# Sorted rows and normalised rows turned by VectorE behind block-wise loads, in a fused convolution-attention and expert-routing kernel

## The chip, the cores and the metric

The kernel runs on one core of one Trainium2 chip. The metric is the device time of one execution in microseconds (us). TensorE multiplies and transposes matrices into PSUM; VectorE, ScalarE and GpSimd work elementwise; SyncE issues most of the DMA transfers that move data between DRAM and SBUF; 16 DMA engines carry them. In profile rows these engines are called PE (with PEld for its weight loads), DVE, ACT, POOL and SP.

## The reference

The input `x` has 4 images of 32 channels, 128 x 128. Everything is float32.

Layer 0 is a channel attention. Each image becomes a matrix q of 128 channels by 4096 places:

```python
xs = x.reshape(B, C, h, R, w, R).transpose(0, 1, 3, 5, 2, 4).reshape(B, C * R * R, h, w)   # R = 2
...
energy = jnp.einsum('bci,bcj->bij', q, q)
d = jnp.sqrt(jnp.diagonal(energy, axis1=1, axis2=2))
energy = energy / (d[:, :, None] * d[:, None, :])
attn = jax.nn.softmax(energy, axis=-1)
out = jnp.einsum('bcj,bij->bci', q, attn).reshape(B, C * R * R, h, w)
out = gamma * out + xs
```

Layer 1 reads the result as tokens of 128 values. The linear attention and the experts follow, each on layer-normalised tokens and each added to the tokens:

```python
t = t + _L1_attn_ref(_ln_t(t), L1_attn_Wk, L1_attn_Wq, L1_attn_Wv)
t = t + _L1_ffn_ref(_ln_t(t), L1_ffn_router_w, L1_ffn_router_b, L1_ffn_expert_w, L1_ffn_expert_b)
```

`_L1_ffn_ref` is a router with a softmax over 8 experts; each token takes the best two, multiplies by each one's 128 x 128 weights and adds the two results, weighted.

## The kernel before

The four images are worked off one after the other. `attend` walks over the 4096 x 4096 matrix of an image in blocks of 128 x 512. Each step has a product for the energies (`pe`, line 609), an exponential by ScalarE (`pr`, L612), a product of the exponential with values (`po`, L497) and, since the matrix is symmetric, a product of the transposed block (`pg`, L433). The transposed block is made without TensorE: VectorE turns `pr` in squares of 32 x 32 (L421, tile `F`), the block goes to DRAM (`move`, L530, tensor `blocks`) and comes back with its 32-row groups swapped (`swap_groups`, L545, `F<-blocks`, six DMAs). The product with it is given out 57 units of a clock after the swap (`LAG`), where one whole step counts 12 units.

Layer 1 of image b is worked in the gaps of the attention of image b + 1. It is written as Python generators (`layer1`): each `yield` is a half step, and the main loop takes one half step of that stream for every 10 units of the clock (`PACE`). So the order of instructions on TensorE, VectorE, ScalarE and SyncE is fixed by the program, and every engine works its own list from top to bottom.

Parts of layer 1 that matter here, for images 0 to 2:

- `close_rows(kc)`, four groups of 8 token rows: divides by the sums, adds to the tokens `T`, normalises them into `xn` (L696) and adds up their Gram matrix (`pgram`, L728). `stagger` starts a group every 6 half steps. The first group waits until the layer 1 of the image before is `sorted`.
- `matrix()`: makes one 128 x 144 matrix, `matx`, of the attention weights and the Gram matrix.
- `attention_rows(u)`, four groups: TensorE transposes the normalised rows, four 128 x 128 tiles at a time, into PSUM (`transpose_rows`, `ptx`, L701), ScalarE copies them out (`keep_rows`, `xnT`, L714), and TensorE multiplies them with `matx` (`pat`, L854). Then come the second normalisation and the router.
- `sorted_experts(h)`, for each half of an image: GpSimd scatters the normalised tokens to a DRAM tensor `xs` sorted by expert, with each token's weight in column 128 (L1053; rows are `DW` = 132 wide), in `NT` = 39 tiles of 128 tokens. The tiles are loaded in pairs (L1083), transposed by TensorE (`pys`, L1124), copied out by ScalarE (L1093), multiplied by their expert's weights (L1117), scaled with the token's weight by VectorE (L1099) and stored to `ys` (L1103). GpSimd then gathers the two results of each token (L1165).

Image 3 has no successor to hide in: it takes another way through layer 1 (`alone`, `last_parts`), with dense experts and with `transpose_rows`, too. The same tile tag names one set of buffers: `wide` and `grp` have two each.

TensorE's PSUM banks are handed out by `hold`, which gives back the function that empties the bank.

Of the kernel before, what the change touches and what calls it, by code (L numbers as in the profile page):

```python
# [22 lines left out]
def kernel(  # L23
# [43 lines left out]
    nc = tc.nc  # L67
    P = 128
# [3 lines left out]
    CH = 512  # L72
# [4 lines left out]
    S = 32  # L77
    NH, KQ, D = wk.shape
# [40 lines left out]
    DW = D + 4  # L119
# [71 lines left out]
    def hold(name, evict, alloc=psum_t):  # L191


        while len(held) >= banks[0]:
            held[0]()
        bank = alloc(name)

        def done():
            if done in held:
                held.remove(done)  # L200
                evict(bank)

        held.append(done)
        return bank, done
# [449 lines left out]
    def layer1(b, st):  # L654
# [43 lines left out]
        def transpose_rows(g):  # L698
            pt, done = hold(f"ptx_{b}_{g}", partial(keep_rows, g))
            for j in range(4):  # L700
                nc.tensor.transpose(pt[:, ts(j, P)], xn[:, 4 * g + j, :D], ident)  # L701
            return done

        def keep_rows(g, pt):

            if not alone:
                xnT = work.tile([P, CH], F32, tag="grp", name=f"xnT_{b}_{g}", bufs=2)
            else:
                nm = f"xnT_{b}_{g}"
                if g in (0, 2, 6):  # L710
                    pool, tag = (xin, "xx") if g == 0 else (qpool, "qT")
                    keep["two"] = pool.tile([P, 2, CH], F32, tag=tag, name=nm)
                xnT = npool.tile([P, CH], F32, tag="qn", name=nm) if g in (4, 5) else keep["two"][:, g % 2]
            nc.scalar.activation(xnT, pt, AF.Copy)  # L714
            keep[g] = xnT

# [14 lines left out]
        def close_rows(kc):  # L731
# [9 lines left out]

            while "exps" not in st if last_rows else missing():
                yield from idle(1)
            while b > 0 and kc == 0 and not states[b - 1].get("sorted"):
                yield from idle(1)
            den, rd = (stat.tile([P, 2 * NJ], F32, tag=nm, name=f"{nm}_{b}_{kc}") for nm in ("den", "rd"))
            nc.vector.tensor_reduce(den, st["sums"][:, ts(kc, 2 * NJ), :], AX.X, ALU.add)
# [174 lines left out]
        def transpose_tokens(g, alloc=psum_t):  # L922
# [7 lines left out]
                nc.tensor.transpose(pt[:, ts(j, P)], xn[:, 4 * g + j, :D], ident)  # L930
            return done

        def attention_rows(u):

            for g in (2 * u, 2 * u + 1):
                yield
                done = transpose_rows(g)
                yield
                done()
            la = stat.tile([P, 8, 2 * E], F32, tag="la", name=f"la_{b}_{u}")  # L940
            for j0 in range(0, 8, 3):
# [24 lines left out]
            if u % 2:  # L966
                for _ in route(u // 2):
                    yield
                    yield
                yield  # L970
                yield
                yield from sorted_experts(u // 2)

        def sorted_experts(h):
# [104 lines left out]
            def rows_of(dram_rows, g, n):  # L1079
                return dram_rows[2 * g * P : (2 * g + n) * P, :].rearrange("(j p) d -> p j d", p=P)  # L1080
# [6 lines left out]
            def products(turned, applied):  # L1087


                def leave(p):  # L1090
                    if turned:
                        g, n = turned
                        nc.scalar.activation(  # L1093
                            bufs[6 + g % 2][:, :n, :D], p[:, : n * P].rearrange("p (j t) -> p j t", t=P), AF.Copy
                        )
                    if applied:
                        g, n = applied
                        result = keep["results"][:, g % 4]
                        nc.vector.tensor_tensor(  # L1099
                            result[:, :n], p[:, 2 * P : 2 * P + n * D].rearrange("p (j c) -> p j c", c=D),  # L1100
                            bufs[g % 6][:, :n, D : D + 1].to_broadcast([P, n, D]), ALU.mult,
                        )
                        nc.sync.dma_start(rows_of(ys, g, n), result[:, :n])  # L1103

                p, done = hold(f"pys_{b}_{h}_{(turned or applied)[0]}", leave)
                if applied:
                    g, n = applied
                    if g % 2 == 0:
                        _, at = nc.values_load_multi_w_load_instructions(
                            begin[0:1, h, 2 * g : min(2 * g + 4, NT)], engines=[mybir.EngineType.PE], min_val=0,  # L1110
                            max_val=(E - 1) * D,
                            skip_runtime_bounds_check_because="D times a count of at most E - 1, never negative",
                        )
                        begins[:] = at
                    weights = ew_sb.rearrange("p e c -> p (e c)")
                    for j in range(n):
                        nc.tensor.matmul(  # L1117
                            p[:, 2 * P + j * D : 2 * P + j * D + D], bufs[6 + g % 2][:, j, :D],
                            weights[:, bass.ds(begins[2 * (g % 2) + j], D)], start=True, stop=True,
                        )  # L1120
                if turned:
                    g, n = turned
                    for j in range(n):
                        nc.tensor.transpose(p[:, ts(j, P)], bufs[g % 6][:, j, :D], ident)  # L1124
                return done

            if "results" not in keep:
                keep["results"] = work.tile([P, 4, 2, D], F32, tag="df", name=f"results_{b}", bufs=1)
            done = None
            begins = []  # L1130
            for at in range(len(pairs) + 5):
                if at < len(pairs):
                    load(*pairs[at])
                if done:
                    done()
                yield
                turned, applied = (pairs[at - d] if 0 <= at - d < len(pairs) else None for d in (3, 4))
                done = products(turned, applied) if turned or applied else None
                yield
            if done:  # L1140
                done()
            if h == 1:
                st["sorted"] = True
            yield from idle(1)
# [353 lines left out]
```

## Time and profile before

| What | Value |
|---|---|
| median of 3 runs | 1652.24 us (1652.22 to 1652.25) |
| the profiled execution's own time | 1659.2 us |
| its span, first to last instruction | 1657.4 us |
| TensorE busy | 1623.1 us, 98% of the span |
| VectorE busy | 917.4 us, 55% |
| ScalarE busy | 910.4 us, 55% |
| GpSimd busy | 596.2 us, 36% |
| DMA packets | 241899, 332.81 MB |
| packets under 512 bytes | 31984 |
| granted clock of TensorE, mean | 0.996 |

A group row of the profile names a line of the kernel, the engine, the operation, `out<-in` by tile names, the shapes and the count. After the bar stand the busy time in us (overlapping instructions counted once), the mean ns of one instruction, and the time that the engine was idle just before, with what ended it. A row of the waits reads: who waited, for whom, us in total, times, longest. The page's strips of 40 digits cut the span into 40 slices, with tenths of busy time. A window row gives, for a stretch of time, each engine's busy us and number of instructions.

### The profile page before, as it was taken

How to read it: one execution, taken by the hardware profiler on the slowest of the kernel's cores; microseconds unless marked ns; L12 is line 12 of the kernel's file. 1: busy time of each engine (PE TensorE's matmuls, PEld its weight loads, DVE VectorE, ACT ScalarE, POOL GpSimd, SP SyncE). 2: the span in 40 equal slices, each digit the busy share in tenths (PEclk: the TensorE clock that was granted, in tenths of full speed). 3: DMA queues.
4: the chain of work that ended last, by engine and by line, in shares of the span. 5: the costliest groups of instructions: out<-in, count | busy, mean ns of one | idle time of the engine just before them, and what ended most of it. 6: DMA issues, size and time to landing. Idle time of an engine off the chain costs nothing.

```text
span 1657.4 us, 21471 instructions
## 1 busy us (share of the span) xinstructions
PE 1623.1 (98%) x5288; PEld 856.9 (52%) x5288; DVE 917.4 (55%) x2359; ACT 910.4 (55%) x2863; POOL 596.2 (36%) x565
## 2 busy tenths in 40 slices
PE   8999999999999999999999999999999999999987
PEld 5444544455554455555564455555565445554643
DVE  4543353567486443559378453448559533344686
ACT  3555445566575555556575455556657455555376
POOL 1000000001014531456555543346546642436166
PEclk9999999999999999999999999999999999999999
DMA  4555656665349776986778868797668877885001
GB/s 147 199 181 174 198 186 213 230 212 170 131 171 277 246 220 213 271 249 176 207 200 254 265 208 255 214 287 200 167 196 239 277 222 246 240 254 168 15 14 39
DMA packets 241899, 332.81 MB, mean 201 GB/s; under 512 B 31984, under 2 KB 168304, under 8 KB 227440
## 3 DMA queue, kind: packets, MB, share of 16 engines
q1 hardware_dynamic: 207312, 291.92, 55.5%
q0 software_dynamic: 26624, 25.58, 7.5%
q10 hardware_dynamic: 7840, 13.93, 2.8%
q8 instruction: 45, 0.74, 0.2%
q14 instruction: 78, 0.64, 0.1%
HBM read 160.78 MB, written 175.80 MB: 203 GB/s over the span
## 4 chain that ended last, share of the span: by engine, by line
PE 84%; DMA 4%; DVE 4%; SPq 3%; ACT 2%; issue 2%; another core or an unknown queue 1%; POOL 0%; ACTq 0%; DVEq 0%; POOLq 0%
PE po L497 24%; PE pe L609 23%; PE pg L433 20%; PE pys L1117 3%; DMA blocks<-F 3%; PE py L1290 3%; PE pg L453 2%; SPq L545 2%; PE pat L854 2%; PE pys L1124 2%; PE pgram L728 1%; PE ptx L701 1%; DVE df L761 1%; PE pgv L839 0%
## 5 line engine op out<-in xcount | busy, mean ns | idle before, releaser
L612 ACT ACTIVATE pr<-pe 128x512 f32<-128x512 f32 (+1 forms) x576 | 322.4, 560 | 544.0 <-PE pe L609 448.2
L497 PE MATMUL po<-pr,qT 128*128 128x512 f32 (+3 forms) x1152 | 549.6, 559 | 4.2 <-ACT o L502 3.0
L609 PE MATMUL pe<-qn,qn 128*128 128x512 f32 x896 | 459.6, 595 | 2.6 <-ACT pr L612 1.6
L433 PE MATMUL pg<-F,qT 128*128 128x512 f32 x880 | 449.7, 592 | 1.1 <-DMA F<-blocks 1.1
L421 DVE STREAM_TRANSPOSE F<-pr 128x512 f32<-128x512 f32 x440 | 305.9, 702 | 144.8 <-ACT pr L612 127.0
L497 PEld LDWEIGHTS po<-pr,qT 128*128 128x128 f32 x1152 | 215.3, 190 | 251.7 <-issue 221.2
L1165 POOL DMA_INDIRECT acc<-ys,place x128 | 203.2, 1588 | 215.8 <-ACT pr L612 140.3
L438 ACT ACTIVATE junk<-F 128x512 bf16<-128x512 f32 x440 | 273.0, 620 | 1.2 <-DMA F<-blocks 1.2
L433 PEld LDWEIGHTS pg<-F,qT 128*128 128x128 f32 x880 | 166.7, 190 | 195.4 <-issue 181.0
L1053 POOL DMA_INDIRECT xs<-xn,place x192 | 186.0, 969 | 189.7 <-ACT pr L612 116.6
L609 PEld LDWEIGHTS pe<-qn,qn 128*128 128x128 f32 x896 | 155.0, 191 | 115.0 <-issue 104.6
L442 DVE TENSOR_TENSOR o<-o,pg 128x512 f32<-128x512 f32 x110 | 75.3, 684 | 207.9 <-PE pg L433 173.4
L1099 DVE TENSOR_TENSOR results<-pys,xn 128x256 f32<-128x256 f32 x120 | 49.9, 416 | 187.1 <-ACT xn L1093 122.0
L164 POOL TENSOR_TENSOR rn<-ss,neg_half 128x8 f32<-128x8 f32 (+1 forms) x17 | 27.2, 1602 | 320.9 <-DVE ss L296 320.8
L612 ACT ACTIVATION_READ_ACCUMULATOR pr<-pe 128x1 f32 x576 | 112.0, 194 | 0.0
L1093 ACT ACTIVATE xn<-pys 128x256 f32<-128x256 f32 x120 | 45.2, 377 | 112.5 <-PE pys L1124 94.5
L1117 PEld LDWEIGHTS pys<-ew_sb,xn 128*128 128x128 f32 x468 | 70.4, 191 | 53.0 <-issue 49.5
L1165 POOL DMA_INDIRECT yb<-ys,place x64 | 61.8, 965 | 84.5 <-DMA F<-blocks 31.1
L609 PE MATMUL pe<-qn 128*128 128x512 f32 (+3 forms) x256 | 90.2, 435 | 0.7 <-ACT qn L342 0.7
L438 ACT ACTIVATION_READ_ACCUMULATOR junk<-F 128x1 f32 x440 | 84.6, 192 | 0.0
L1117 PE MATMUL pys<-ew_sb,xn 128*128 x468 | 71.7, 275 | 0.4 <-ACT xn L1093 0.4
L164 POOL TENSOR_TENSOR rsa<-dm_a,neg_half 128x8 f32<-128x8 f32 x16 | 28.9, 1807 | 103.1 <-DVE sv_a L688 102.9
(216 smaller groups left out, 1521.1 us busy)
## 6 DMA issues: line engine op xcount, KB each, us to landing
blocks<-F SPq DMA_DIRECT2D x110, 1024.0 KB
F<-blocks SPq DMA_DIRECT2D x220, 192.0 KB
F<-blocks SPq DMA_DIRECT2D x220, 128.0 KB
xn<-xs SPq DMA_DIRECT2D x114, 132.0 KB
ys<-results SPq DMA_DIRECT2D x114, 128.0 KB
F<-blocks SPq DMA_DIRECT2D x220, 64.0 KB
below<-F SPq DMA_DIRECT2D x31, 384.0 KB
T<-in_x_dram SPq DMA_DIRECT2D x64, 128.0 KB
```

What stands on the lines that cost most here:

```text
L164: pinned(nc.gpsimd.tensor_tensor(dst, src, neg_half.to_broadcast(list(src.shape)), ALU.pow))
L421: f()
L433: nc.tensor.matmul(pg.rearrange("p (a f) -> p a f", a=4), st["qT"][i][:, ib, :], G[:, :, ib], start=(ib == 0), stop=(ib == NJ - 1),)
L438: nc.scalar.activation(junk, G[:, :, ib], AF.Copy, accum_out=st["sums"][:, NJ * i + ib, jc : jc + 1])
L442: nc.vector.tensor_tensor(st["o"][jc], st["o"][jc], pg, ALU.add)
L497: nc.tensor.matmul(row["po"][:, lo:hi], qT[blk // NJ][:, blk % NJ, :], w, start=start, stop=(row["left"] == 0))
L609: nc.tensor.matmul(pe[:, c0:], qn[jc][:, ts(j, P)], qn[i][:, c0:], start=True, stop=True)
L612: nc.scalar.activation(pr[:, c0:], pe[:, c0:], AF.Exp, accum_out=sums[:, t, i : i + 1]).ins
L1053: inst = nc.gpsimd.indirect_dma_start(xs[h], offset(place[:, i, k : k + 1]), xn[:, k, :], None)
L1099: nc.vector.tensor_tensor(result[:, :n], p[:, 2 * P : 2 * P + n * D].rearrange("p (j c) -> p j c", c=D), bufs[g % 6][:, :n, D : D + 1].to_ ...
L1117: nc.tensor.matmul(p[:, 2 * P + j * D : 2 * P + j * D + D], bufs[6 + g % 2][:, j, :D], weights[:, bass.ds(begins[2 * (g % 2) + j], D)], st ...
L1165: inst = nc.gpsimd.indirect_dma_start(to, None, ys, offset(place[:, i, k : k + 1]), compute_op=op)
```

## The change

For images 0 to 2, the normalised rows go to DRAM after each `close_rows` group (`rows`, one DMA of 512 KB). `fetch_blocks` brings them back with four DMAs for each group of 8 rows, each moving one 32-column stripe into one group of 32 partitions, in runs of 32 values. `attention_rows` turns them with two VectorE instructions, in squares of 32 x 32, and the result is the transposed tile that TensorE and ScalarE made before. The fetch for group u + 1 is issued when group u begins.

In `sorted_experts`, tiles are taken by four. `load` uses four DMAs with the same pattern of 32-value runs, `turn` is one VectorE instruction for four tiles, `product` multiplies four tiles into one PSUM bank, and its eviction scales all four and stores them with one DMA. The weights of all tokens of a half are loaded with one DMA (`factor`, single values of 4 bytes). In a loop of half steps, tile group g is loaded at step 4g, turned at 4g + 8, multiplied at 4g + 11 and evicted at 4g + 13. The loop has 50 half steps, as before.

`close_rows` has new conditions: every group waits for `sorted`, group kc starts only when group kc - 2 has been added to `T`, and takes its bank only when group kc - 1 has. `keep_rows` loses its branch for images 0 to 2; image 3 still uses it.

```diff
@@ close_rows
-            while b > 0 and kc == 0 and not states[b - 1].get("sorted"):
+            added = st.setdefault("added", set())
+            while b > 0 and not states[b - 1].get("sorted") or kc > 1 and kc - 2 not in added:
                 yield from idle(1)
...
+            while kc > 0 and kc - 1 not in added:
+                yield
             pb, done = hold(f"pbd_{b}_{kc}", divide)
...
             nc.vector.tensor_tensor(tk, tk, df.rearrange("p k w r -> p k (w r)"), ALU.add)
+            added.add(kc)
...
+            if not alone:
+                rows = dram.tile([P, 8, D], F32, tag="rows", name=f"rows_{b}_{kc}", bufs=4)
+                nc.sync.dma_start(rows, xn[:, ts(kc, 8), :D])
+                keep["rows", kc] = rows
@@ attention_rows
+        def fetch_blocks(u):
+
+            keep["blocks", u] = blocks = work.tile([P, 8, D], F32, tag="wide", name=f"blocks_{b}_{u}")
+            for q in range(4):
+                nc.sync.dma_start(
+                    blocks[ts(q, S)].rearrange("i k (a c) -> i k a c", c=S),
+                    keep["rows", u][:, :, ts(q, S)].rearrange("(a i) k c -> i k a c", i=S),
+                )
+
         def attention_rows(u):
 
+            if u < 3:
+                fetch_blocks(u + 1)
+            yield
             for g in (2 * u, 2 * u + 1):
-                yield
-                done = transpose_rows(g)
-                yield
-                done()
+                keep[g] = work.tile([P, CH], F32, tag="grp", name=f"xnT_{b}_{g}", bufs=2)
+                nc.vector.transpose(keep[g], keep["blocks", u][:, ts(g % 2, 4), :].rearrange("p k d -> p (k d)"))
+                yield
+            yield
@@ sorted_experts
-            bufs = [xn[:, r0 + 2 * i : r0 + 2 * i + 2, :] for i in range(8)]
-            pairs = [(g, min(2, NT - 2 * g)) for g in range((NT + 1) // 2)]
...
-            def load(g, n):
-                inst = nc.sync.dma_start(bufs[g % 6][:, :n], rows_of(xs[h], g, n))
...
-                if turned:
-                    g, n = turned
-                    for j in range(n):
-                        nc.tensor.transpose(p[:, ts(j, P)], bufs[g % 6][:, j, :D], ident)
...
+            room = xn[:, half, :].rearrange("p k w -> p (k w)")
+            parts = [room[:, 4 * DW * i : 4 * DW * i + 4 * D] for i in range(4)]
+            quads = [(g, min(4, NT - 4 * g)) for g in range((NT + 3) // 4)]
+            factor = stat.tile([P, NT, 1], F32, tag="factor", name=f"factor_{b}_{h}")
...
+            def load(g, n):
+                rows = xs[h][4 * g * P : (4 * g + n) * P, :D].rearrange("(m i) w -> i m w", i=S)
+                for q in range(4):
+                    read(
+                        nc.sync.dma_start(
+                            parts[g % 2][ts(q, S), : n * D].rearrange("i (m c) -> i m c", c=S), rows[:, :, ts(q, S)]
+                        )
+                    )
+
+            def turn(g, n):
+                nc.vector.transpose(parts[2 + g % 2][:, : n * D], parts[g % 2][:, : n * D])
+
+            def product(g, n):
 
                 def leave(p):
...
+                    result = keep["results"][:, ts(g % 2, 4)]
+                    nc.vector.tensor_tensor(
+                        result[:, :n], p[:, : n * D].rearrange("p (j c) -> p j c", c=D),
+                        factor[:, 4 * g : 4 * g + n].to_broadcast([P, n, D]), ALU.mult,
+                    )
...
+                for j in range(n):
+                    nc.tensor.matmul(
+                        p[:, ts(j, D)], parts[2 + g % 2][:, ts(j, D)],
+                        weights[:, bass.ds(begins[j], D)], start=True, stop=True,
+                    )
                 return done
...
+            read(nc.sync.dma_start(factor, xs[h].rearrange("(t p) w -> p t w", p=P)[:, :, D : D + 1]))
+            leaves = {}
+            for at in range(4 * len(quads) + 10):
+                for first_at, act in ((8, turn), (0, load), (11, product), (13, lambda g, n: leaves.pop(g)())):
+                    if at >= first_at and (at - first_at) % 4 == 0 and (at - first_at) // 4 < len(quads):
+                        g, n = quads[(at - first_at) // 4]
+                        made = act(g, n)
+                        if act is product:
+                            leaves[g] = made
+                yield
@@ all_parts
             yield from stagger([close_rows(kc) for kc in range(4)], 3)
+            fetch_blocks(0)
             yield from matrix()
```

More of the change, by code (lines that the diff above doesn't have):

```diff
@@ L704, in keep_rows @@
         def keep_rows(g, pt):
[L706 to L713, printed above, removed]
+            nm = f"xnT_{b}_{g}"
+            if g in (0, 2, 6):
+                pool, tag = (xin, "xx") if g == 0 else (qpool, "qT")
+                keep["two"] = pool.tile([P, 2, CH], F32, tag=tag, name=nm)
+            xnT = npool.tile([P, CH], F32, tag="qn", name=nm) if g in (4, 5) else keep["two"][:, g % 2]
             nc.scalar.activation(xnT, pt, AF.Copy)
@@ L1073, in sorted_experts @@
             yield from idle(3)
-            bufs = [xn[:, r0 + 2 * i : r0 + 2 * i + 2, :] for i in range(8)]
-            pairs = [(g, min(2, NT - 2 * g)) for g in range((NT + 1) // 2)]
-            def rows_of(dram_rows, g, n):
-                return dram_rows[2 * g * P : (2 * g + n) * P, :].rearrange("(j p) d -> p j d", p=P)
-            def load(g, n):
-                inst = nc.sync.dma_start(bufs[g % 6][:, :n], rows_of(xs[h], g, n))
+            room = xn[:, half, :].rearrange("p k w -> p (k w)")
@@ L1084, in load, with read @@
+            parts = [room[:, 4 * DW * i : 4 * DW * i + 4 * D] for i in range(4)]
+            quads = [(g, min(4, NT - 4 * g)) for g in range((NT + 3) // 4)]
+            factor = stat.tile([P, NT, 1], F32, tag="factor", name=f"factor_{b}_{h}")
+            def read(inst):
                 wait_for(inst.ins, xs_made[h], "a tile holds tokens of any row")
                 xs_read[h].append(inst.ins)
-            def products(turned, applied):
-                def leave(p):
-                    if turned:
-                        g, n = turned
[L1093 to L1115, printed above, removed]
-                    for j in range(n):
[L1117 to L1124, printed above, removed]
@@ new lines, in product @@
+            def product(g, n):
+                def leave(p):
+                    result = keep["results"][:, ts(g % 2, 4)]
[3 more added lines that the diff above has]
+                    )
+                    nc.sync.dma_start(
+                        ys[4 * g * P : (4 * g + n) * P, :].rearrange("(j p) d -> p j d", p=P), result[:, :n]
+                    )
+                p, done = hold(f"pys_{b}_{h}_{g}", leave)
+                _, begins = nc.values_load_multi_w_load_instructions(
+                    begin[0:1, h, 4 * g : 4 * g + n], engines=[mybir.EngineType.PE], min_val=0,
+                    max_val=(E - 1) * D,
+                    skip_runtime_bounds_check_because="D times a count of at most E - 1, never negative",
+                )
+                weights = ew_sb.rearrange("p e c -> p (e c)")
+                for j in range(n):
+                    nc.tensor.matmul(
+                        p[:, ts(j, D)], parts[2 + g % 2][:, ts(j, D)],
+                        weights[:, bass.ds(begins[j], D)], start=True, stop=True,
+                    )
@@ L1125, in products @@
                 return done
             if "results" not in keep:
[L1128 to L1135, printed above, removed]
-                yield
-                turned, applied = (pairs[at - d] if 0 <= at - d < len(pairs) else None for d in (3, 4))
-                done = products(turned, applied) if turned or applied else None
-                yield
@@ L1140, in sorted_experts @@
-            if done:
-                done()
+                keep["results"] = work.tile([P, 8, D], F32, tag="df", name=f"results_{b}", bufs=1)
+            read(nc.sync.dma_start(factor, xs[h].rearrange("(t p) w -> p t w", p=P)[:, :, D : D + 1]))
[7 more added lines that the diff above has]
+                            leaves[g] = made
+                yield
```

## The prediction, made before the changed kernel was run

> **What bounds the kernel now.** I read the page's busy times first, then the groups of instructions with their shapes kept apart, then who waits for whom, then busy times by stage, then a stretch of the matmul engine's timeline. The page:
>
> ```profile
> PE 1623.1 (98%) x5288; PEld 856.9 (52%) x5288; DVE 917.4 (55%) x2359; ACT 910.4 (55%) x2863; POOL 596.2 (36%) x565
> ...
> DMA  4555656665349776986778868797668877885001
> ...
> PE po L497 24%; PE pe L609 23%; PE pg L433 20%; PE pys L1117 3%; DMA blocks<-F 3%; PE py L1290 3%; PE pg L453 2%; SPq L545 2%; PE pat L854 2%; PE pys L1124 2%; PE pgram L728 1%; PE ptx L701 1%; DVE df L761 1%; PE pgv L839 0%
> ```
>
> TensorE works from the first slice to the last; every other engine has some 40% or more to spare. So an instruction taken from TensorE pays its full time, as long as nothing new makes TensorE wait. It hardly waits now; its waits for data that travelled through DRAM are these:
>
> ```profile
> PE pg L433 <- DMA F<-blocks: 1.1, 1, 1.1
> ```
>
> The rows that the change touches (last figures: busy us, mean ns of one, idle before):
>
> ```profile
> L1124 PE MATMUL pys<-ident,xn 128*128 128x128 f32 x234 | 45.1, 273 | 0.0
> ...
> L701 PE MATMUL ptx<-ident,xn 128*128 128x128 f32 x128 | 20.1, 285 | 2.2 <-ACT xnT L714 1.4 <-DVE df L761 0.8
> ```
>
> 273 ns is how long one transpose is in flight, not what it costs: matmuls overlap. The timeline gives the cost:
>
> ```profile
> 704.17 1.02 PE L433 MATMUL pg<-F,qT 128*128 128x512 f32 x2
> 705.03 0.61 PE L1117 MATMUL pys<-ew_sb,xn 128*128 x4
> 705.48 0.38 PE L1124 MATMUL pys<-ident,xn 128*128 128x128 f32 x2
> 705.70 1.02 PE L609 MATMUL pe<-qn,qn 128*128 128x512 f32 x2
> ```
>
> From 705.48 to 705.70 two transposes occupy 0.22 us: 0.11 us each.
>
> The stages, in the trace's busy times by stretch: sorted rows of image 0's halves (586:653, 665:731) and of image 1's second half; the third column from the end is the granted clock, then DMA share and GB/s:
>
> ```profile
> 586.00:653.00 67.00, 67.00 (x254) 38.15 (x253) 25.87 (x52) 34.70 (x108) 20.91 (x23) 1.00 0.72 225
> 665.00:731.00 66.00, 66.00 (x248) 36.99 (x247) 31.53 (x60) 34.16 (x104) 32.76 (x22) 1.00 1.00 275
> ...
> 1053.00:1120.00 67.00, 67.00 (x251) 37.46 (x250) 31.87 (x62) 34.25 (x105) 33.64 (x22) 1.00 1.01 274
> ```
>
> VectorE is half idle there; the DMA engines are full in the second halves, which also carry the gathers of the first. This is where the change can fail.
>
> **Removed from TensorE.** 234 transposes of sorted rows (39 tiles x 2 halves x 3 images) and 96 of the 128 of L701 (image 3 keeps 32). Taking the time from the end of the instruction before to its own end, they hold TensorE for 25.6 and 10.5 us, 109 ns each. Sum: 36.0 us, all on the path. The products L1117 stay, 234 in 468 passes. Here a rule speaks against the change: the Trainium skill, "VectorE: DVE Perf Modes", section "The three transpose paths", prices a 128x128 bf16 transpose at 390 ns on TensorE and 311 ns on VectorE, which turns 32x32 blocks only, and its rules advise TensorE. At 390 ns the gain would be 129 us; among other matmuls the trace shows 109 ns, so I use 36.0. That VectorE turns only blocks is why the loads must rearrange, with runs of 128 bytes.
>
> **Moved to VectorE.** 60 turns of 128x512 for sorted rows and 24 for attention, nearest L421 (`F<-pr`, 702 ns): 59 us. The 120 evictions by L1099 (49.9 us) become 60 of 128x512; nearest L442 (684 ns): 41 us. VectorE goes to about 917 + 59 - 9 = 967 us, 60% of the new span, and to about half of each stage. ScalarE loses L1093 (45.2 us) and 24 of 32 evictions of L714 (14 us). Nothing of either lies on the path.
>
> **New waits.** Each turn waits for its load, given out 8 half steps earlier. Half steps are some 1.6 us apart (20 pair steps of two half steps fill the 63 us from 586 to 649), so 12.6 us; before, the transpose had 6 half steps, 9.4 us. Behind a late turn VectorE queues the turns of F and the additions to o, for which SP's block moves and then TensorE wait. On SP, every block load from the third on waits for the turn two groups back, given out in the same half step; behind it stand the moves of F. In attention the second turn of a group waits for attention products one half step later: under 2 us of VectorE, nine times. Cover for all of these: matching DMA packets to issues in order, the last packet of an F swap lands 3.2 us (worst after 300 us) to 18 us, mostly 6 to 12, before its first use. A delay below that costs nothing; one above it reaches TensorE at once. The changed conditions in `close_rows` keep groups in sequence; TensorE's order of image 3's last 190 rows is unchanged, so I give them 0.
>
> **SP.** Removed: 120 tile loads, 60 of 120 stores of results. Added: 240 loads of sorted blocks, 48 of attention blocks, 12 row stores, 6 loads of factors. Net +126 issues on 1541; at 0.43 us (median of L1083) 54 us, about 5 us per half of some 66 us. SP's issues fill about 32 of 50 us in the dense stretches, so they fit; a wait falls on the next swap and has the same cover.
>
> **DMA.** The page shows no 128-byte packet. The trace's packet records, sorted by size, do bound it: medians of 9 ns for 4 bytes (completions), 9 for 32 bytes (router weights), 27 for 512, 28 for 528, 36 for 768, 84 for 2048, 311 for 8192. That is 8 ns plus 0.037 ns per byte; 128 bytes come to 13 ns. Bounds: 9 ns, and 27 ns, the 512-byte packet. A rule again speaks against: the Trainium skill, "DMA: Bandwidth & Descriptors", section "Specifications", says that under 512 bytes the engine reads, modifies and writes. Packets that really do so here, the accumulating gathers of L1165, take 65 ns; at 65 ns 119,808 + 49,152 packets over 16 engines are 686 us and the kernel is far slower. The 32-byte loads at 9 ns show no such price, so I keep 13.
> Per half: 19,968 x 13 / 16 = 16.2 us of blocks, 4,992 factors of 4 bytes at 9 ns 2.8 us, less 4,992 rows at 28 ns, 8.7 us: +10.3 us. Two second halves with a share of 1.00 and 6 us of cover: at most 2 x 4.3 = 8.7 us of stall; but a packet's recorded time includes its waiting, and at uncontended medians the share is about 0.85 there, which makes it 0. First halves: 67 x 0.28 = 19 us free, 0. Image 2 (136 us at 0.79, 29 us free for 20.6): 0. Attention, per image: 16,384 x 13 / 16 = 13.3 us of blocks and 4,096 x 27 / 16 = 6.9 us of row stores, these spread over the earlier closing steps, beside 38 us at shares 0.41, 0.69 and 0.72: 0. So 0 to 9 us; I take the middle with a little for SP, 5 us.
>
> **Sum.** The profiled execution has a span of 1657.4 us (1659.2 with what lies around it), 5.2 us above the median of 1652.24. Span: 1657.4 - 36.0 + 5 = 1626; the same 31 us from the median: **1621 us**.
>
> **Rivals.**
> *A. Small packets cost about as much as 512-byte ones; the DMA engines become the bound.* For: share 1.00 in the second halves, and the page counts 128-byte packets nowhere. Against: the straight line above. At c ns a half adds 1.25c - 6 us. At 27 ns (factors included, 8.4 us) that is 33: second halves stall 33 - 6 = 27 each, first ones 33 - 25 = 8 each, image 2 67 - 35 = 32, attention about 20; together 122. 1616 + 122 = 1738. It decides from about c = 20 ns, where the same sum gives 35 us and eats the gain. Slower.
> *B. SP gets late.* Its order is fixed, and it now stops at VectorE's turns 48 times. For: SP already loses 215.2 us to `SPq L545 <- DMA blocks<-F`. Against: 6 to 12 us of usual cover. If a third of the stops cost TensorE 1 us: 1621 + 16 = 1637.
> *C. No change:* stalls happen to equal 36 us, c near 20 ns: 1652.
> *D. Cover holds everywhere:* 1616.
>
> **Numbers.** Likeliest case with D 0.55, own range 1612 to 1630; B 0.17 (1630 to 1648); C 0.04; A 0.24 (1656 to 1750). The measurement tells 0.2% (3.3 us) from no change. Faster 0.72, same 0.04, slower 0.24. Up to 1630 and B, C are 0.76 together; to leave out no more than 0.2 the range takes in the near part of A: 1611 to 1680.
>
> **What would show it.** TensorE's count down by 330, its busy time near 1587 us and still 98%; L1124 gone, L701 at x32; turns near 700 ns; waits of TensorE for `F<-blocks` still a few us. 128-byte packets at 13 ns and a DMA share up some 0.08. It is wrong if `PE pg <- DMA F<-blocks` or waits for VectorE's turn reach tens of us, above all at 660 to 735 and 1050 to 1120, or if SP's waits for DMA grow by more than 50 us.

## The result: 0.4% slower, and the profile after

The kernel before took 1652.22 us (median of 7 runs), the changed kernel 1658.05 us (7 runs, 1654.3 to 1661.48): ratio 1.0038, 95% interval 1.0028 to 1.0048. The forecast was 1621 us, 31 us less than before; the kernel became 6 us slower. The profiled execution of the changed kernel took 1661.48 us, with a span of 1659.7 us and a mean granted clock of 0.991 (before: 1659.2, 1657.4 and 0.996).

The page of the changed kernel, the rows that answer to those shown of before:

```profile
PE 1596.7 (96%) x4958; PEld 823.6 (50%) x4958; DVE 958.0 (58%) x2383; ACT 856.0 (52%) x2719; POOL 590.4 (36%) x565
...
DMA  4654656666759798996899789898698899896001
...
DMA packets 425158, 344.98 MB, mean 208 GB/s; under 512 B 232912, under 2 KB 351568, under 8 KB 410704
...
PE po L497 23%; PE pe L609 22%; PE pg L433 19%; PE py L1301 3%; DMA F<-blocks 3%; PE pys L1134 3%; PE pg L453 2%; SPq L545 2%; DMA acc<-t 2%; PE pgram L725 1%; DMA blocks<-F 1%; PE pat L859 1%; ACT pr L612 1%; ACT xn L696 1%; DVE F L421 1%
```

TensorE has its 330 instructions less, but its busy share fell from 98% to 96%. In the chain, `DMA F<-blocks` and `DMA acc<-t` have come in, which the chain of before did not list. The groups with their shapes kept apart:

```profile
L1134 PE MATMUL pys<-ew_sb,xn 128*128 x468 | 62.3, 276 | 5.3 <-DVE xn L1112 5.3
...
L1112 DVE STREAM_TRANSPOSE xn<-xn 128x512 f32<-128x512 f32 x54 | 37.2, 689 | 57.9 <-DMA xn<-xs 57.8
L1118 DVE TENSOR_TENSOR results<-pys,factor 128x512 f32<-128x512 f32 x54 | 36.6, 678 | 21.1 <-DMA ys<-results 16.8 <-PE pys L1134 4.1
...
L701 PE MATMUL ptx<-ident,xn 128*128 128x128 f32 x32 | 4.6, 277 | 2.2 <-ACT xnT L711 1.4 <-DVE df L759 0.8
```

A turn takes 689 ns and an eviction 678 ns, as costed. New is the idle time: VectorE stood 57.8 us in front of turns whose load had not landed, and TensorE 5.3 us for turns. TensorE's waits:

```profile
PE pg L433 <- DMA F<-blocks: 14.8, 10, 2.4
PE pgram L725 <- DVE gram L719: 5.7, 2, 2.9
PE pys L1134 <- DVE xn L1112: 5.3, 4, 3.8
PE pe L609 <- ACT pr L612: 4.6, 3, 1.6
PE pbd L774 <- DVE rdx L750: 2.0, 2, 1.0
```

The first was 1.1 us before, the fourth 1.6, the others absent: 29.7 us of new waits. A view of the same trace puts the gain and the loss side by side. For every TensorE instruction take the time from the end of the one before it to its own end; the median of each kind of instruction is its usual step, what lies above is a stall. How kinds of instruction are told apart moves these sums by up to 1 us.

| us | before | after | difference |
|---|---|---|---|
| sum of usual steps | 1597.2 | 1562.8 | -34.4 |
| above the usual steps | 50.1 | 86.7 | +36.6 |

So the gain is there, and it was given back in stalls. Only 29.7 us of these are waits. The rest is clock: between 100 and 1560 us the waits of 2 us and more are seven, and with five of them the record of the granted clock shows 0.5 (from 759 us for 6.83 us, from 855, 1090, 1158 and 1476 for 3.41 each). Leaving out the last few microseconds of the span, the clock is at half for 27.3 us, before for 10.2; half of the difference, 8.5 us, is lost, as the mean clock says too (0.991 for 0.996 of 1660 us).

Why do swaps come late? The waits of SP's queue, of before and then of after:

```profile
SPq L545 <- DMA blocks<-F: 215.2, 64, 6.1
SPq L530 <- DMA acc<-t: 39.2, 9, 9.6
SPq L1103 <- DMA acc<-t: 17.8, 3, 6.2
SPq L1159 <- DMA acc<-t: 11.5, 2, 5.8
```

```profile
SPq L545 <- DMA blocks<-F: 252.7, 76, 7.2
SPq L545 <- DMA acc<-t: 34.1, 9, 7.2
SPq L530 <- DMA acc<-t: 30.6, 4, 9.6
SPq L1106 <- DMA acc<-t: 28.4, 5, 7.4
```

`acc<-t` is no transfer of SP's: it is the fetch of attention results for the gathers, 24 in all, issued by ScalarE (L1163; L1153 before). The trace names the semaphore of every issue: the DMAs of SP and ScalarE count on the same eight (100 to 107). Each of the 18 waits for `acc<-t` (14 before) stands in front of an issue of SP that waits for the semaphore it is to use, and the last DMA on that semaphore was a fetch of ScalarE's. A fetch that lands late therefore holds SP, and all that stands behind in SP's list. Before, that fell on block moves, stores and outputs, 68.5 us in all; now, of 93.1 us, it falls nine times on swaps (L545) and five times on loads of sorted blocks (L1106). One case on the timeline of the changed kernel, engines in the order of time:

```profile
844.47 0.34 ACTq L1163 DMA_DIRECT2D acc<-t  x1
...
849.12 0.32 SPq L545 DMA_DIRECT2D F<-blocks  x1
...
854.33 1.71 PE L433 MATMUL pg<-F,qT 128*128 128x512 f32 x2 [2.11 <-DMA F<-blocks]
855.83 1.91 PE L609 MATMUL pe<-qn,qn 128*128 128x512 f32 x2
```

The trace's waits of SP between 844 and 850 us hold one row, `SPq L545 <- DMA acc<-t: 3.9, 1, 3.9`: ScalarE issues the fetch at 844.47, SP stands 3.9 us, the next part of the swap goes out at 849.12, and TensorE stands 2.11 us. The two rows at the end take 1.71 and 1.91 us, where a pair of such matmuls takes 1.02: that is the half clock, from 854.7 us on. The last packet of this swap landed 0.8 us before its first use, and TensorE waited all the same: a cover of about 1 us, counted by packets as below, is none.

The cover of a swap (last packet landed to first use, from DMA packets matched to issues) in the two second halves of sorted rows:

| kernel | swaps issued at 660 to 745 us: median cover | at 1050 to 1135 us | least after 300 us |
|---|---|---|---|
| before | 6.8 us | 7.1 us | 3.2 us |
| after | 1.1 us | 1.0 us | 0.5 us |

These are medians of six or seven swaps each. A swap still takes 5 to 6 us from issue to landing there. It is issued 7.0 us ahead of its use instead of 12.8.

### The profile page after: what moved, and what is told of

Its sections match the earlier page's. It is cut to its first block, busy times and chain, and to the rows that moved or that the text cites. A ratio compares the mean times of both kernels' runs of the same rounds, so it can differ in the third digit from the quotient of the medians.

```text
span 1659.7 us, 20613 instructions
## 1 busy us (share of the span) xinstructions
PE 1596.7 (96%) x4958; PEld 823.6 (50%) x4958; DVE 958.0 (58%) x2383; ACT 856.0 (52%) x2719; POOL 590.4 (36%) x565
## 3 DMA queue, kind: packets, MB, share of 16 engines
q1 hardware_dynamic: 390576, 304.15, 63.3%
## 4 chain that ended last, share of the span: by engine, by line
PE 76%; DMA 8%; DVE 7%; SPq 3%; ACT 3%; issue 2%; POOL 1%; ACTq 0%; DVEq 0%; POOLq 0%
PE po L497 23%; PE pe L609 22%; PE pg L433 19%; PE py L1301 3%; DMA F<-blocks 3%; PE pys L1134 3%; PE pg L453 2%; SPq L545 2%; DMA acc<-t 2%; PE pgram L725 1%; DMA blocks<-F 1%; PE pat L859 1%; ACT pr L612 1%; ACT xn L696 1%; DVE F L421 1%
## 5 line engine op out<-in xcount | busy, mean ns | idle before, releaser
L433 PE MATMUL pg<-F,qT 128*128 128x512 f32 x880 | 452.3, 596 | 14.8 <-DMA F<-blocks 14.8
L609 PEld LDWEIGHTS pe<-qn,qn 128*128 128x128 f32 x896 | 160.4, 192 | 144.4 <-issue 130.9
L1134 PEld LDWEIGHTS pys<-ew_sb,xn 128*128 128x128 f32 x468 | 61.3, 192 | 32.4 <-issue 25.7
L1112 DVE STREAM_TRANSPOSE xn<-xn 128x512 f32<-128x512 f32 (+1 forms) x60 | 40.5, 676 | 62.9 <-DMA xn<-xs 62.7
L1134 PE MATMUL pys<-ew_sb,xn 128*128 x468 | 62.3, 276 | 5.3 <-DVE xn L1112 5.3
L1301 PE MATMUL py<-ew_sb,xn 128*128 128x512 f32 x128 | 61.4, 622 | 5.2 <-ACT tmp L1257 4.0
```

Of the source, the lines that this page charges most:

```text
L433: nc.tensor.matmul(pg.rearrange("p (a f) -> p a f", a=4), st["qT"][i][:, ib, :], G[:, :, ib], start=(ib == 0), stop=(ib == NJ - 1),)
L609: nc.tensor.matmul(pe[:, c0:], qn[jc][:, ts(j, P)], qn[i][:, c0:], start=True, stop=True)
L1134: nc.tensor.matmul(p[:, ts(j, D)], parts[2 + g % 2][:, ts(j, D)], weights[:, bass.ds(begins[j], D)], start=True, stop=True,)
L1301: nc.tensor.matmul(bank, xn[:, k, :D], ew_sb[:, 4 * h : 4 * h + 4, :], start=True, stop=True)
```

## The experiments

The twelve kernels ran in three groups, e1 to e4, e5 to e8 and e9 to e12, each on another chip; the kernel before takes 1659.8 to 1660.5 us there, and each ratio is to the kernel before on the same chip. The table is for reference below; "stalls" is the profiled TensorE time above usual steps.

| kernel | median us | ratio to before, 95% | stalls us |
|---|---|---|---|
| e1 sorted part alone | 1673.32 | 1.0072 (1.0051 to 1.0092) | 87.1 |
| e2 attention part alone | 1664.06 | 1.0015 (1.0002 to 1.0028) | 65.0 |
| e3 old conditions | 1672.56 | 1.0082 (1.0051 to 1.0112) | 98.9 |
| e4 long runs | 1660.85 | 1.0002 (0.9992 to 1.0013) | 88.6 |
| e5 changed kernel again | 1677.86 | 1.0097 (1.0070 to 1.0125) | 101.6 |
| e6 filler | 1698.83 | 1.0223 (1.0195 to 1.0252) | 86.3 |
| e7 later use | 1700.40 | 1.0243 (1.0208 to 1.0278) | 122 |
| e8 fetch by GpSimd | 1641.78 | 0.9896 (0.9855 to 0.9937) | 62.2 |
| e9 before, fetch by GpSimd | 1662.37 | 1.0010 (1.0003 to 1.0017) | 51.9 |
| e10 fetch by GpSimd, long runs | 1633.68 | 0.9835 (0.9818 to 0.9851) | 61.3 |
| e11 fetch by GpSimd, filler | 1667.82 | 1.0046 (1.0029 to 1.0063) | 54.2 |
| e12 fetch by GpSimd again | 1646.38 | 0.9909 (0.9891 to 0.9927) | 73.3 |

**Which part: e1 and e2.** e1 has the kernel before with the new `sorted_experts` only; e2 has the rows through DRAM only, with the old sorted rows and conditions. For e1, against the changed kernel:

```diff
-            if not alone:
-                rows = dram.tile([P, 8, D], F32, tag="rows", name=f"rows_{b}_{kc}", bufs=4)
...
-                nc.vector.transpose(keep[g], keep["blocks", u][:, ts(g % 2, 4), :].rearrange("p k d -> p (k d)"))
+                done = transpose_rows(g)
```

> The kernel before with only the sorted rows loaded by blocks and turned by VectorE; attention rows and the conditions of close_rows as before. TensorE loses 234 transposes, 25.6 us. If the lost gain sits where the changed kernel's TensorE waits in its own sorted stages (about 20 us more than before by the trace), this run is at 1652 - 25.6 + 20 = 1647 us, and the stalls at 488, 757, 882 and 1154 us are gone. If DMA is near its limit only because both parts load it, it is near 1630. If SyncE's queue is upset by the extra issues everywhere, it is above 1652.

> The kernel before with only the normalised rows turned through DRAM and VectorE; sorted rows and the conditions of close_rows as before. TensorE loses 96 transposes, 10.5 us. If each part pays for itself but for its own stalls (some 10 us in the attention stages), 1652 us. If attention rows cost nothing new on their own, 1642. If their 512-row DMAs hold SyncE up, above 1655.

Usual steps fell to 1572.7 us with the sorted part and to 1587.6 with the attention part: 24.5 and 9.6 us, so both gains are real. Both kernels are slower than before all the same. The sorted part does most of the harm (+12 us by the ratio though 24.5 of work are gone); this is the last case of its expectation, above 1652, and the stalls near 757 and 1154 us did not go (two waits of 2.4 us at 763 and 1153). The attention part is near neutral (+2.5 us, the interval just off 1): about the first case, each part pays for its own stalls. The two losses add up: 0.72% and 0.15% make 0.87%, and e5 with both parts shows 0.97% on another chip.

**The conditions in `close_rows`: e3.**

```diff
-            while b > 0 and not states[b - 1].get("sorted") or kc > 1 and kc - 2 not in added:
+            while b > 0 and kc == 0 and not states[b - 1].get("sorted"):
...
-            while kc > 0 and kc - 1 not in added:
-                yield
```

> The changed kernel with the conditions of close_rows as before. If the waits of pbd and pgram at 757 and 1154 us (7.1 and 6.0 us over the usual time in their stretches of 50 us) come from the conditions, it gains 12 us: 1646. If they come from the shorter time between half steps or from late work on VectorE, it stays within 3 us of 1658.

1.0082 against 1.0097 for e5 on another chip; the intervals overlap, so no effect is shown in either direction, and the 12 us of the first case did not come. The stall near 760 and 1155 us only moves from the Gram product to the product before it. The row of this kernel, to be held against `PE pgram L725 <- DVE gram L719: 5.7, 2, 2.9` of the changed one:

```profile
PE pbd L771 <- DVE gram L719: 4.9, 2, 2.4
```

**Short packets: e4.** Both loads fetch whole rows, 512 bytes a run, with as many DMAs and the same bytes.

```diff
-                rows = xs[h][4 * g * P : (4 * g + n) * P, :D].rearrange("(m i) w -> i m w", i=S)
+                rows = xs[h][4 * g * P : (4 * g + n) * P, :D].rearrange("(m p) w -> p m w", p=P)
...
-                    blocks[ts(q, S)].rearrange("i k (a c) -> i k a c", c=S),
-                    keep["rows", u][:, :, ts(q, S)].rearrange("(a i) k c -> i k a c", i=S),
+                    blocks[ts(q, S)],
+                    keep["rows", u][ts(q, S)],
```

> The changed kernel with block loads in runs of 512 bytes in place of 128: as many DMAs and bytes, a quarter of the packets. It leaves the rearrangement of the blocks out, so the values that it computes are others. If small packets are what makes SyncE and the swaps late (issues of L1106 take 688 ns in the mean where 425 are usual), issues fall to about 430 ns and half of the 37 us of stalls goes: 1640. If the wait for a semaphore shared with ScalarE's fetch of acc, or the pace, is what counts, it stays at 1650 to 1658.

This leaves the rearrangement of blocks out of the computation. It came to the time of before, not below it: some 1% better than e5, measured on another chip, and the 36 us still not won. Short packets look like a part of the loss and not the whole. The mean issue of L1106 fell only from 689 to 628 ns, not to 430, and SP's waits for `acc<-t` stayed (101.4 us in all, of it 29.2 at L530, 26.1 at L545, 17.6 at L1106). So small packets alone do not explain the loss, and the shared semaphores came under suspicion.

**The changed kernel once more, and what a transpose is worth: e5 and e6.** e6 adds 330 transposes of the identity where the old ones were; their results are overwritten. Shown is the part for the sorted rows; the attention rows get 96 of them in the same way.

```diff
+                for j in range(n):
+                    nc.tensor.transpose(p[:, ts(j, D)], ident, ident)
                 for j in range(n):
                     nc.tensor.matmul(
```

> The changed kernel itself, on the chip of the three runs beside it, to have its ratio there: 1.004 of the kernel before, as first measured.

> The changed kernel with 330 transposes of the identity put on TensorE where the transposes taken away had stood (in front of the products of the sorted rows and of the attention rows, into the bank that the products overwrite): TensorE's work is that of the kernel before again, everything else is the changed kernel's. If TensorE's removed time had been the cover of late data (pace theory), the stalls shrink by nearly what the filler costs and the time stays within 10 us of the changed kernel's. If the stalls come from SyncE and DMA whatever TensorE does, 36 us are added: ratio to before about 1.025.

On this chip the changed kernel is 18 us slower than before, more than the 6 us of the first pair, so e5's expectation was missed. Of TensorE's waits, e5 and then e6:

```profile
PE po L497 <- ACT o L502: 12.1, 14, 8.7
PE pg L433 <- DMA F<-blocks: 11.3, 9, 2.6
```

```profile
PE pe L609 <- ACT pr L612: 17.4, 6, 7.9
...
PE pg L433 <- DMA F<-blocks: 2.8, 3, 1.5
```

In e5's trace two late stalls are in part to blame, which the first profile of the changed kernel lacks (8.7 us up to 1451 us of a product that waits for ScalarE's `o`, 4.6 at 1523 us with nothing named). They are no accident of one trace: such pairs, between 1430 and 1546 us, stand in every kernel here that has the new sorted rows with fetches on ScalarE (e1 9.9 and 6.3, e3 9.9 and 3.0, e4 4.2 and 3.1, e6 5.6 and 7.9, e7 10.4 and 9.2), save that first profile; with the fetches on GpSimd, below, the longest wait of such a product there is 3.3 us. What they come from stays open: in e5 TensorE, VectorE and ScalarE all stand from 1442 to 1447 us, while GpSimd works and the DMA engines are full.

The filler costs 21 us where its usual steps cost 34.6 us (1597.5 against 1562.9), so neither case of its expectation came true: the changed kernel has room between its stalls. With the same count of TensorE instructions as before, e6 takes 39 us longer than the kernel before: that is the price of the new arrangement by itself, as long as ScalarE issues the fetches.

**More time for the swaps: e7.** The product with a swapped block is given out 69 units after the swap instead of 57.

```diff
-    LAG = 57
+    LAG = 69
```

> The changed kernel with the product of a transposed block given out 69 instead of 57 units of the clock after its swap, one whole step (some 2 us) later. If swaps that come late by up to 2.4 us are what costs (14.8 us of waits for F<-blocks and the half clock after them, some 20 us), the ratio falls from 1.004 to 0.992. If the waits for ScalarE and VectorE are what costs, it falls by less than 0.004.

The ratio was to fall and rose, to 1.0243. TensorE's waits in this kernel:

```profile
PE pe L609 <- ACT pr L612: 20.7, 9, 9.2
PE pbd L774 <- DVE rdx L750: 14.2, 6, 5.6
...
PE pg L433 <- DMA F<-blocks: 8.4, 4, 4.4
PE pys L1134 <- DVE xn L1112: 7.4, 5, 2.9
```

Waits for swaps fell from 11.3 (e5) to 8.4 us only, and those for VectorE and ScalarE grew by more. Later use also holds the tiles `F` longer and shifts the order on every engine, so this run says little about the cover; it does say that a delay chosen to fit one order is no free cushion.

**The suspected wait itself: e8.** The 24 fetches go out from GpSimd, whose DMAs count on eight other semaphores (111 to 118).

```diff
-                nc.scalar.dma_start(accs[g], t2[:, ts(g, 4)])
+                pinned(nc.gpsimd.dma_start(accs[g], t2[:, ts(g, 4)]))
```

> The changed kernel with the 24 fetches of acc issued by GpSimd in place of ScalarE, so that SyncE's DMAs no longer take turns with them on the same semaphores. If SyncE's 93 us of waits for acc<-t (34.1 of them at swaps) are the main cause of late swaps, TensorE's waits for F<-blocks fall below 5 us and the ratio falls to about 0.993. If the issue of many small packets is, less than 0.003 is gained.

1641.78 us: 36 us below e5 on the same chip, and 1.0% below the kernel before. SP's waits of this kernel hold no row for `acc<-t`; TensorE's hold none for `pg <- F<-blocks` (11.3 us in e5). Of SP's and of TensorE's waits:

```profile
SPq L545 <- DMA blocks<-F: 209.9, 63, 6.8
SPq L1106 <- DMA blocks<-F: 0.2, 1, 0.2
```

```profile
PE pe L609 <- ACT pr L612: 9.0, 5, 3.3
PE pgram L725 <- DVE gram L719: 5.7, 2, 2.9
```

**The control: e9.** The same edit in the kernel before.

> The kernel before, with nothing changed but that the 24 fetches of the attention result (acc <- t) are issued by GpSimd instead of ScalarE. In the trace of before SP stands 68.5 us for acc <- t, and TensorE's time above its usual steps is 50 us. Theory (SP's order loses to ScalarE's fetches only where the extra transfers make those waits fall on swaps): the fetches cost the kernel before little, because its swaps land 3 us or more ahead of their use; ratio 0.994 to 1.000, SP's waits for acc <- t gone, few us of TensorE won. Rival (moving the fetches is a gain by itself and has nothing to do with the change): ratio 0.985 to 0.992, as much as the changed kernel won by it.

1.0010: no gain, 2 us of loss, a little above the 0.994 to 1.000 of the theory and far from its rival. SP's waits for the fetches, 68.5 us before, are gone here too, and nothing is won: before, they fell on moves, stores and outputs. So what e8 won is not a gain that was lying about in both kernels: it is what the changed kernel lost by meeting these fetches. The edit does more than part the semaphores: it takes the fetches, 0.33 us each to issue, out of ScalarE's list, and the first goes out at 631 us where in e5 it goes at 653. e9 rules these out as gains by themselves; which of them the changed kernel lives on was not tested apart. Its size is less sure than its cause: stalls fell by 39.4 us from e5 to e8, and e5's two late ones, 13.3 us together, are among them; against the first profile of the changed kernel (86.7 us) e8 has 24.5 us less.

**What remains, with that cause removed: e10, e11, e12.** e12 is e8 again, to compare with on this chip; e10 adds the edit of e4, e11 that of e6.

> The changed kernel with the fetches issued by GpSimd, and its sorted and attention blocks loaded in runs of 512 bytes instead of 128; this leaves the rearrangement of the blocks out of the computation, the turns and products stay. It prices the 128-byte packets once SP no longer stands for ScalarE's fetches. Theory (packets of 13 ns are not a bound): the same time as with short runs, within 0.4%. Rival (the full DMA queues still delay something): 0.5% to 1% below the run with short runs of this call.

> The changed kernel with the fetches issued by GpSimd, and 330 transposes of the identity put back on TensorE in the places of those removed (their results are overwritten by the products). Theory (TensorE is the bound again once SP's waits are gone, each transpose costs 109 ns of the path): 30 to 36 us above the run without them, ratio to before 1.006 to 1.012. Rival (the loose stalls absorb part of it): 10 to 22 us above, as the 21 us that the same transposes cost in the changed kernel itself.

> The changed kernel with the 24 fetches of the attention result issued by GpSimd, once more, as the base of this call. Theory: the ratio of its first measurement, 0.9896, again; 0.985 to 0.994. If that was luck of one chip: 0.996 or more.

e12 repeats e8: 0.9909. Two rivals won here. Short packets do cost something, 12.7 us between e12 and e10; and the filler again costs 21.4 us, not 36. Two sums follow. With the filler, the changed kernel stands 39.0 us above before when ScalarE issues the fetches (e6) and 7.5 us when GpSimd does (e11). And with both causes out, fetches and short runs, the kernel is 26.7 us below before (e10, which leaves the rearrangement out), near the 31 us of the forecast.

How 13-ns packets cost 12.7 us can be followed to VectorE. VectorE's waits for loads and TensorE's for VectorE, of e12 and then of e10:

```profile
DVE xn L1112 <- DMA xn<-xs: 22.4, 11, 3.2
...
PE pgram L725 <- DVE gram L719: 5.7, 2, 2.9
```

```profile
DVE xn L1112 <- DMA xn<-xs: 3.3, 4, 1.0
...
PE pgram L725 <- DVE gram L719: 1.8, 2, 1.3
```

With short runs the turns wait for their loads, VectorE comes out of the sorted stage with a backlog, and the copy of the first Gram sum (L719), which is at the end of an unbroken row of VectorE's work at 744 to 753 us, is 2.87 us late; the clock is at 0.5 for 6.83 us from 753 us. This links the two waits by their order in the trace; it was not tested by itself, and e4, with long runs and the fetches on ScalarE, keeps the 5.7 us at the Gram sum.

The filler shows something else. Median cover of swaps in the same two stretches of time:

| kernel | 660 to 745 us | 1050 to 1135 us |
|---|---|---|
| e5 changed | 1.1 us | 1.2 us |
| e6 changed, filler | 2.1 us | 2.4 us |
| e8 changed, fetch by GpSimd | 3.1 us | 2.4 us |
| e9 before, fetch by GpSimd | 8.8 us | 8.1 us |
| e11 changed, fetch by GpSimd, filler | 8.4 us | 7.7 us |
| e12 changed, fetch by GpSimd | 2.5 us | 2.4 us |
| e10 the same, long runs | 4.4 us | 6.0 us |

e11 and e12 issue the same DMAs in the program's order. There the transposes alone make the difference between 8.4 and 2.5 us. Where TensorE gets faster it comes sooner to each use, while SP and the DMA engines have the same work as with the filler (DMA share 1.06 in e11 and 1.08 in e12 at 665 to 731 us): the cover shrinks, by 5.9 us where the half itself became 3.8 us shorter. But pace is only one of two: with the fetches on ScalarE the same transposes bring back 1 us (e5 to e6), and the fetches moved without transposes 1 to 2 us (e5 to e8); both together bring back some 7 (e11). Against e11, e12 lost 19.1 us in stalls (73.3 against 54.2), most of it at 750 to 800 us (6.7 against 1.5) and 1100 to 1150 us (7.1 against 0.8), the Gram stalls and their clock, and from 1300 to 1500 us (9.4 against 2.7). The second halves themselves lost nothing: from first to last product 56.7 us against 60.5.

The version that beats both kernels with the full computation is e8/e12.

## Why the prediction was wrong, step by step

The range that went with the forecast, 1611 to 1680 us, holds 1658 only by luck: its upper part was put there for rival A, small packets as dear as 512-byte ones, and 13 ns rules that out.

- **Removed from TensorE, 36.0 us at 109 ns each: right.** Usual steps fell by 34.4 us. The 390 ns of the Trainium skill ("VectorE: DVE Perf Modes", "The three transpose paths") is not what a transpose costs among matmuls here.
- **Moved to VectorE: right in size.** Busy 958.0 us for 967, turns at 689 ns for 702. "Nothing of either lies on the path" was wrong: TensorE waited twice for the Gram copy (5.7 us) and four times for a turn (5.3 us).
- **DMA: packets right, their effect under-sized.** 168,960 packets of 128 bytes have a median of 13 ns (mean 14.3), and queue 1's share went from 55.5% to 63.3%, the predicted 0.08. The rule of reading, modifying and writing under 512 bytes (the Trainium skill, "DMA: Bandwidth & Descriptors", "Specifications") does not show in these loads: plain packets of 128 and 512 bytes take 13 and 27 ns, the accumulating gathers of 512 bytes 65. Rival A is out in the form given. The term was put at 0 to 9 us, of which I took 5 with SP; with the fetches out of the way the short runs alone cost 12.7 us (e10 against e12). The DMA share of the second halves is 1.08 and 1.09 in e12, 1.00 in e10, so full engines are not ruled out as the reason why loads come late.
- **SP: +126 issues right, 54 us wrong.** In the trace SP's 1541 DMA instructions last 713.5 us before, its 1667 last 875.3 after: +162 us. One load of sorted blocks takes 689 ns in the mean (median 487, longest 4.6 us), one of attention blocks 1053 (median 708), where I took 430 for each. That was a median: the mean of L1083 was 569 ns already before. With a quarter of the packets (e10 against e12) the medians fall from 491 to 435 and from 682 to 420, the mean of the first only from 716 to 653: part of the price is the number of packets.
- **The cover: the step that failed.** "Cover for all of these ... 3.2 us ... to 18 us, mostly 6 to 12 ... A delay below that costs nothing", and for SP "a wait falls on the next swap and has the same cover". The 6 to 12 us were those of a kernel whose TensorE was 36 us slower and whose SP met ScalarE's fetches on other transfers. In the stretches that mattered they became 1 us, and delays of SP reached TensorE: 14.8 us of waits for `F<-blocks` where 1.1 had been. SP's 162 us of dearer issues do not use the cover up by themselves: e11 has them too, and a cover of 8.4 us. I priced each delay singly against a cover that the change itself was using up.
- **What SP waited for.** Rival B, "SP gets late", was the right mechanism with the wrong stopper, and 0.17 of the chance. It named SP's stops at VectorE's turns, and gave 16 us. The stopper was the fetch of `acc` in ScalarE's list, 68.5 us of SP's waits in the profile of before, harmless there (e9), which I had not read. Moved away, the changed kernel gains 36 us on one chip (e8 against e5; 24.5 us in stalls against its first profile) and the kernel before none: of what went wrong and was measured, this is the largest part.
- **Stalls cost more than their length: not counted.** With five of seven waits came 3.4 us of half clock or a multiple; half clock costs 8.5 us more than before.
- **`close_rows` at 0: not contradicted** (e3).
- **The signs named beforehand** mostly came true: TensorE's count, turns, packets, share, and, as the signs of failure, 14.8 us of waits for `F<-blocks`, a busy share of 96%, and SP's waits for `blocks<-F` and `acc<-t`, which grew by 62 us (283.7 to 345.8).

Not settled: what the two late stalls are, and why the changed kernel has them on two chips and not in its first profile, which goes far to explain 1.0% against 0.4% (e5 has 15 us more of stalls); the kernel before differs by 0.5% between these chips too.

## What to carry to other kernels

Cover is measured in the time of the engine that is being made faster: subtract at least the gain, stretch by stretch, from the cover of every transfer that this engine uses (here a stretch 3.8 us shorter lost 5.9 us of cover), and take off what the change puts into the issuing queue, before calling a delay hidden. Read the waits of the issuing queue in the profile of before, also those that cost nothing there: a wait for another engine's DMA is harmless only until new instructions move it onto a transfer that is needed. And when a real gain vanishes, put the removed work back as filler: what it costs and what the cover becomes tell how much of the old balance hung on it.

## What the runs showed of the hardware

A 128-byte packet takes 13 ns, a 512-byte one 27 ns, so the four short ones that carry the same bytes take 52. The issue of a DMA by SP grows with its packets: 682 against 420 ns in the median for attention blocks of 1024 and 256 packets (e12 and e10). The longest issues of sorted blocks, some 4 us, come with either length of run. In the changed kernel's profile a wait of TensorE of 2 to 4 us is mostly (five of seven) joined by 3.41 or 6.83 us at half of the granted clock, an 8.7 us one in e5 by 10.24; but in e8 only one of three is. So the wait of 2.1 us at 854 us costs, as an estimate from these 3.41 us, some 1.7 us on top. SP's and ScalarE's DMAs share eight semaphores in these programs, and a fetch of ScalarE's held SP for up to 9.6 us; GpSimd's use eight others.
